# A post-LayerNorm transformer layer with eight experts: results scattered to token rows, side steps dealt by counted DVE work, POOL and SP in emission order, LayerNorm stores from ACT

## The chip, the core and the metric

The kernel runs on one core of one Trainium2 chip. The metric is the device time of one execution in microseconds (us); several executions were timed and their median is given. One further execution was recorded by the hardware profiler; its page and its trace are what is read here. PE is the tensor engine, DVE the vector engine, ACT the scalar engine, POOL is GpSimd and SP the engine that mostly issues DMAs. "SPq" is the queue of SP's sequencer.

## The reference

The input holds 16 sequences of 512 tokens with 128 features. All arithmetic is float32.

```python
Q, K, V = heads(x @ Wq.T + bq), heads(x @ Wk.T + bk), heads(x @ Wv.T + bv)   # 16 heads of 8
probs = softmax(Q @ K.T / sqrt(8))
intervened = probs.at[:, :, :, 0].set(0.0); intervened /= intervened.sum(-1)
attn = ((probs + 0.5 * (intervened - probs)) @ V) @ Wo.T + bo
x1 = layernorm(x + attn)                              # no scale, no shift
logits = x1 @ gate_w.T                                # 8 experts
w, selected = phi_routing(logits)                     # two experts and two weights a token
moe = sum over e of wte[:, e] * ((silu(x1 @ w1[e].T) * (x1 @ w3[e].T)) @ w2[e].T)   # F = 512
out = layernorm(x1 + moe)
```

## The kernel before

**Turns.** A sequence ("batch" b) takes 32 turns (UNITS). A turn n handles one pair of score blocks. `scores` writes transposed scores into a pair of PSUM banks: L388 adds the negated row maxima by a bf16 matmul, L393 adds the products of queries and keys. `exponentials` (L404, ACT) makes `ex` from them, and `weighted` (L413, PE) multiplies `ex` with the values. The row maxima are made LEAD = 20 turns ahead: `maxima` (L338, PE) computes the scores a first time in another pair of banks, and `reduce_maxima` (L346, DVE) reduces them to `nm`. Every 16 turns `put_maxima` splits 16 turns' `nm` into bf16 pieces, transposes them and stores them from `mT` to the operand `mt` (L372).

**Side steps.** Everything else of the attention is written as Python generators that are walked a step further in each turn, up to a `yield`: `load_x`, `project` (queries and keys, high and low parts `hi` and `lo`, stored to `qrow` and `krow` in DRAM, L290), `load_operands` (loads `qt` and `kt`, L322), `values`, `after_attention` (division by the denominators, output matrix, LayerNorm, store of `x1d` at L468), `route` (logits, the two chosen experts, their weights, and the places of the tokens within the experts' lists) and `finish`. Each generator in the list `active` makes one step a turn; of those that need a PSUM bank of their own (`ONE`) only the first does.

**Experts.** The batches form groups of 3, 4, 4, 3 and 2. `route` ends with eight indirect DMAs per batch (L615), two a turn, that scatter the rows of `x1` into `xg`, ordered by expert. When the last batch of a group is through, `plan` computes from the counts which expert and which rows each tile of 128 rows has, and for every token the row of its two results (`yrow`). `experts` then walks the group's tiles, 163 in all: `fetch` loads the expert's weights `ws` (768 KB, L695) and the rows `xs` (64 KB, L697) three tiles ahead (AHEAD) at addresses read from `plan`'s result; `up` multiplies (L111), `activate` makes `th` and `hT` (L716, L720, L724), and `down_and_turn` multiplies tile j down and transposes tile j+2's rows (L115) into the same bank; ACT copies both to `yx` (L749). Tile j's half goes to `yg` by a DMA from SP:

```python
            if j >= 0:
                nc.sync.dma_start(grp.yg[j * P : (j + 1) * P, :], yx[:, 0, :])
```

**Finish.** When a group's tiles are done, `finish` runs per batch: eight indirect DMAs from POOL (L785), two a turn, gather the two results of each token into `yt`; `xr` is loaded from `x1d`; two DVE operations per quarter (L797, L800) make the weighted sum `z`; then LayerNorm and the store of `out` (L807). LayerNorm (L233 to L251) runs on DVE but for one POOL power (L245, `lnrs`) and the final ACT activations (L251).

**What sets the order.** PE, DVE and ACT execute in the order in which the Python code emits. POOL and SP are ordered by the framework's scheduler, which chose, for instance, to start the copy of the expert weights into one array (`wcat`, three DMAs) near the start of the program although it is emitted in turn 48. How many expert instructions a turn gets is a goal in columns of matmul: what is left of the group, divided by the turns up to its due turn `until` (with CHAIN = 32 and WAIT = 8), plus BASE = 1450. After the last turn ("the tail") only the last group has a goal of its own, half a tile a pass.

Of the kernel before, what the change touches and what calls it, by code (L numbers as in the profile page):

```python
# [33 lines left out]
def post_ln_layer(  # L34
# [78 lines left out]

    def turned(out, src, identity):
        nc.tensor.transpose(out, src, identity)  # L115
        dealt[0] += P
# [43 lines left out]
    nc.vector.tensor_copy(ident_b, ident)  # L160
# [3 lines left out]
    nc.vector.memset(keymask, 1.0)  # L164
    nc.vector.memset(keymask[0:1, :], 0.0)
# [3 lines left out]
    for i in range(2):  # L169
# [3 lines left out]
        nc.vector.tensor_scalar(  # L173
# [5 lines left out]
    for e in range(E):  # L179
        nc.vector.memset(revidx[:, e : e + 1], float(E - e))  # L180
    mhalf = const.tile([P, NT], F32, name="mhalf")
    nc.vector.memset(mhalf, -0.5)
# [5 lines left out]
    def concat_weights():  # L188
        rows = wcat.rearrange("(e p) c -> p e c", p=P)
        nc.sync.dma_start(rows[:, :, 0:F], w1T)  # L190
        nc.sync.dma_start(rows[:, :, F : 2 * F], w3T)
        nc.sync.dma_start(rows[:, :, 2 * F : WROW], w2T.rearrange("p e c d -> p e (c d)"))
# [9 lines left out]

    before = const.tile([P, P], F32, name="before")
# [5 lines left out]
    zeros = const.tile([P, 512], F32, name="zeros")  # L209
# [4 lines left out]
    nc.vector.memset(ones8, 1.0)  # L214
    zero8 = const.tile([P, E], F32, name="zero8")
    nc.vector.memset(zero8, 0.0)
    edge = const.tile([P, JT], F32, name="edge")
    for j in range(JT):
        nc.vector.memset(edge[:, j : j + 1], float(j * P))
    kidx = const.tile([P, KT], F32, name="kidx")  # L220
    for k in range(KT):
        nc.vector.memset(kidx[:, k : k + 1], float(k))
# [3 lines left out]
    nc.vector.tensor_copy(pidx, pidx_i)  # L226
# [5 lines left out]

    def layernorm(dst, z, tag):  # L233
# [3 lines left out]
        for t in range(NT):  # L237
            nc.vector.bn_stats(st[:, t, :], z[:, t, :])
            if t % 2 == 1:
                yield None  # L240
        for t in range(NT):
            nc.vector.bn_aggr(mv[:, t, :], st[:, t, :])
        rs = small.tile([P, NT], F32, tag="lnrs", name=f"lnrs{tag}")
        nc.vector.tensor_scalar_add(rs, mv[:, :, 1], LN_EPS)
        nc.gpsimd.tensor_tensor(rs, rs, mhalf, ALU.pow)  # L245
        yield None
        yield None
        off = small.tile([P, NT], F32, tag="lnoff", name=f"lnoff{tag}")
        nc.vector.scalar_tensor_tensor(off, mv[:, :, 0], -1.0, rs, ALU.mult, ALU.mult)
        for t in range(NT):  # L250
            nc.scalar.activation(  # L251
                dst[:, t, :], z[:, t, :], AF.Identity, bias=off[:, t : t + 1],
# [8 lines left out]
    TURN = "turn"  # L261
    SCORE = 680
# [4 lines left out]
    def project(b):  # L267
# [11 lines left out]
        for i, rows in enumerate(qkrows[b]):  # L279
# [6 lines left out]
            nc.vector.scalar_tensor_tensor(  # L286
# [5 lines left out]
    def values(b):  # L292
# [10 lines left out]
        nc.vector.tensor_tensor(  # L303
# [6 lines left out]
        nc.vector.tensor_scalar(  # L310
# [33 lines left out]
    def reduce_maxima(ks, nm):  # L344

        nc.vector.tensor_reduce(nm, pair(ks), AX.X, ALU.max, negate=True)  # L346
        release(*ks)

    def put_maxima(b, half):

        yield None
        nm = nms.pop((b, half)).rearrange("p t s j -> p t j s")
        pc = small.tile([P, NT, 4, NPC, 2], BF16, tag="pc", name=f"pc{b}_{half}")
        for r in range(NPC):
            nc.vector.tensor_copy(pc[:, :, :, r, :], nm)
            if r < NPC - 1:
                rest = small.tile([P, NT, 4, 2], F32, tag="rest", name=f"rest{b}_{half}_{r}")
                nc.vector.tensor_tensor(rest, nm, pc[:, :, :, r, :], ALU.subtract)
# [628 lines left out]
```

## Time and profile before

| | |
|---|---|
| Time, median of 3 runs | 1698.61 us (1688.18 to 1700.37) |
| Time of the profiled execution | 1850.96 us |
| Span of the profiled execution | 1849.2 us |
| Mean granted TensorE clock in it | 0.850 |
| PE busy | 1457.5 us, 79% of the span |
| DVE busy | 1130.0 us, 61% |
| ACT busy | 854.6 us, 46% |
| POOL busy | 347.1 us, 19% |
| Bytes moved | 276.35 MB, mean 149 GB/s |

The profiled execution is longer than the timed ones. Busy time is the time in which an engine executes instructions; a busy engine is not at its peak. The page cuts the span into 40 slices of about 46 us and gives each engine's busy share in tenths. In the groups, a row has the line, engine and operation, what is written from what, the shape and the count, then busy us in all and mean ns of one, and then the idle time in front of these instructions with what ended most of it. In the list of waits a row has the waiting engine and line, what it waited for, and us in all, how often, and the longest. In the trace the first `ex` starts at 55.84 us, the last turn ends near 1627, and the last result of an expert tile is copied at 1812.4.

### The profile page before, as it was taken

To read this page: it belongs to the slowest core of one execution; us is meant where nothing else is said; L and a number is where in the kernel's file an instruction comes from. 1 tells how busy PE (TensorE), PEld (TensorE's weight loads), DVE (VectorE), ACT (ScalarE), POOL (GpSimd) and SP (SyncE) were. 2 spreads that over 40 slices of the span, in tenths; PEclk is the share of its full clock that TensorE was granted. 3 is DMA by queue.
4 is the path that set the end of the run, shared out by engine and by line. 5 is a ranking of instruction groups with operands and counts; after the bars stand their busy time and mean duration, and the time that the engine had idled before them with its cause. 6 is when DMAs were issued, how large, how long until landed. Compare 5 with 4: busy or idle time off the path is not lost.

```text
span 1849.2 us, 28501 instructions
## 1 busy us (share of the span) xinstructions
PE 1457.5 (79%) x10283; PEld 850.2 (46%) x10283; DVE 1130.0 (61%) x2264; ACT 854.6 (46%) x1270; POOL 347.1 (19%) x352
## 2 busy tenths in 40 slices
PE   4788887778979798788879798888859977977671
PEld 1223232234545454444545454554535545667661
DVE  5656665666767676565657677566656764345342
ACT  1355554545556564354546464454535544432221
POOL 2000102111010101222210101222230014123324
PEclk9557776779999997888879898889988998988996
DMA  8761212245353442445445443455544524556671
GB/s 292 274 228 35 86 45 71 89 138 169 107 171 119 157 143 78 150 138 169 144 139 168 143 150 107 148 170 188 164 134 149 180 94 154 175 172 214 220 247 59
DMA packets 137820, 276.35 MB, mean 149 GB/s; under 512 B 17232, under 2 KB 60496, under 8 KB 137680
## 3 DMA queue, kind: packets, MB, share of 16 engines
q1 hardware_dynamic: 129488, 257.74, 42.8%
q0 software_dynamic: 8192, 16.79, 3.0%
q8 instruction: 81, 1.33, 0.3%
q14 instruction: 59, 0.48, 0.1%
HBM read 195.89 MB, written 84.08 MB: 151 GB/s over the span
## 4 chain that ended last, share of the span: by engine, by line
PE 51%; DVE 20%; issue 9%; ACT 7%; another core or an unknown queue 5%; DMA 4%; POOL 3%; SPq 1%; POOLq 0%; ACTq 0%; DVEq 0%
PE banks L111 22%; PE banks L413 12%; DVE nm L346 10%; PE banks L388 7%; PE banks L338 5%; PE banks L115 4%; ACT ex L404 3%; PE banks L393 2%; POOL yt L785 2%; DMA xs<-xg 1%; DVE th L720 1%; ACT y L251 1%; ACT x L251 1%; DVE hT L724 1%
## 5 line engine op out<-in xcount | busy, mean ns | idle before, releaser
L346 DVE TENSOR_REDUCE nm<-banks 128x2 f32<-128x1024 f32 x512 | 624.5, 1222 | 486.7 <-PE banks L338 321.9
L404 ACT ACTIVATE ex<-banks 128x1024 f32<-128x1024 f32 x512 | 524.1, 1024 | 462.6 <-PE banks L393 358.7
L111 PE MATMUL banks<-yx,ws 128*128 128x128 f32 x2608 | 405.3, 301 | 40.6 <-ACT yx L749 16.5
L111 PEld LDWEIGHTS banks<-yx,ws 128*128 128x128 f32 x2608 | 349.4, 207 | 183.9 <-issue 139.2
L338 PE MATMUL banks<-kt,qt 32*128 32x512 f32 x1024 | 290.6, 568 | 89.0 <-DVE nm L346 61.6
L393 PE MATMUL banks<-qt,kt 32*128 32x512 f32 x1024 | 332.1, 643 | 0.0
L413 PE MATMUL banks<-ex,vaug 128*32 128x512 f32 x2048 | 322.7, 707 | 0.0
L388 PE MATMUL banks<-mt,ones_b 3*128 3x512 bf16 x1024 | 225.4, 434 | 61.8 <-issue 21.0
L615 POOL DMA_INDIRECT xg<-x,sloti x128 | 126.4, 987 | 511.3 <-DVE lo L286 122.0
L111 PE MATMUL banks<-ws,hT 128*128 128x128 f32 x1304 | 194.9, 298 | 5.6 <-ACT aw L431 3.5
L111 PEld LDWEIGHTS banks<-ws,hT 128*128 128x128 f32 x1304 | 184.5, 217 | 10.2 <-ACT aw L431 6.2
L785 POOL DMA_INDIRECT yt<-yg,yrow x128 | 132.3, 1034 | 284.2 <-DVE z L800 89.5
L388 PEld LDWEIGHTS <-ones_b 3*128 3x128 bf16 x1024 | 56.4, 94 | 252.0 <-issue 210.5
L716 ACT ACTIVATE th<-banks 128x512 f32<-128x512 f32 x163 | 97.0, 595 | 159.1 <-PE banks L111 111.8
L338 PEld LDWEIGHTS banks<-kt,qt 32*128 32x128 f32 x1024 | 107.1, 207 | 128.4 <-DVE nm L346 91.2
L724 DVE TENSOR_TENSOR hT<-th,banks 128x512 f32<-128x512 f32 x163 | 111.0, 681 | 62.3 <-PE banks L111 43.7
L720 DVE SCALAR_TENSOR_TENSOR th<-th,banks 128x512 f32<-128x512 f32 x163 | 110.8, 680 | 60.2 <-ACT th L716 57.0
L749 ACT COPY yx<-banks 128x256 f32<-128x256 f32 (+1 forms) x178 | 62.6, 352 | 172.4 <-PE banks L111 131.8
L115 PE MATMUL banks<-ident,xs 128*128 128x128 f32 x163 | 53.4, 328 | 82.9 <-ACT mT L369 29.2
L393 PEld LDWEIGHTS banks<-qt,kt 32*128 32x128 f32 x1024 | 110.0, 211 | 0.0
L413 PEld LDWEIGHTS banks<-ex,vaug 128*32 128x32 f32 x2048 | 42.9, 115 | 87.5 <-issue 86.4
L115 PEld LDWEIGHTS banks<-ident,xs 128*128 128x128 f32 x163 | 24.5, 150 | 126.2 <-ACT mT L369 31.3
(128 smaller groups left out, 1001.4 us busy)
## 6 DMA issues: line engine op xcount, KB each, us to landing
ws<-wcat SPq DMA_DIRECT2D x163, 768.0 KB
qt<-qrow SPq DMA_DIRECT2D x32, 512.0 KB
kt<-krow SPq DMA_DIRECT2D x32, 512.0 KB
xg<-zeros SPq DMA_DIRECT2D x16, 1024.0 KB
xs<-xg SPq DMA_DIRECT2D x163, 64.0 KB
yg<-yx SPq DMA_DIRECT2D x163, 64.0 KB
qrow<-hi SPq DMA_DIRECT2D x32, 256.0 KB
qrow<-lo SPq DMA_DIRECT2D x32, 256.0 KB
```

What stands on the lines that cost most here:

```text
L111: nc.tensor.matmul(out, lhsT, rhs, start=start, stop=stop)
L115: nc.tensor.transpose(out, src, identity)
L338: nc.tensor.matmul(pm[:, u, :], qt[at, s, t * P : (t + 1) * P], kt[at, s, :], start=True, stop=True)
L346: nc.vector.tensor_reduce(nm, pair(ks), AX.X, ALU.max, negate=True)
L388: nc.tensor.matmul(pc[:, u, :], ones_b[at : at + NPC, :], mt[at : at + NPC, g % 2, :], start=True, stop=False,)
L393: nc.tensor.matmul(pc[:, u, :], kt[at : at + HR, g % 2, c * P : (c + 1) * P], qt[at : at + HR, g % 2, :], start=False, stop=True,)
L404: nc.scalar.activation(ex, pair(ks), AF.Exp, scale=SCALE)
L413: nc.tensor.matmul(av[32 * j : 32 * j + 32, :], vas[b][:, c, 4 * g + j, :], ex[j // 2][:, j % 2, :], start=(c == 0), stop=(c == NT - 1),)
L615: put = nc.gpsimd.indirect_dma_start(out=grp.xg, out_offset=bass.IndirectOffsetOnAxis(ap=sloti[:, s, t : t + 1], axis=0), in_=x1[:, t, :], ...
L720: nc.vector.scalar_tensor_tensor(th, th, 1.0, banks[:, ks[0], :], ALU.add, ALU.mult)
L724: nc.vector.tensor_tensor(hT, th, banks[:, ks[1], :], ALU.mult)
L785: nc.gpsimd.indirect_dma_start(out=yt[:, s, t, :], out_offset=None, in_=grp.yg, in_offset=bass.IndirectOffsetOnAxis(ap=grp.yrow[:, i, s, t ...
```

## The change

1. **Results.** The array `yg` and the indices `yrow` are gone. `xg` has two more columns (XW = 130), which POOL copies into `x1`: twice the token's number within the group (`token`), and its first expert. `plan` computes three marks per tile instead. When a tile's rows are turned, two POOL operations make from these columns the row of `yd` that each result belongs to (token times two, plus one where the tile is of the first expert; rows past an expert's count go to places of nobody), and `put_results` scatters the tile by one indirect DMA from POOL. `finish` loads its batch's 512 KB of `yd` by one plain DMA from SP.
2. **Side steps.** All DVE operations of the kernel go through `Counted`, which adds up their free size plus 150 each. A side step is walked when the DVE work emitted so far is less than FULL = 2400 ahead of what the turns have served, or when it has waited more than PATIENCE = 3 turns (1 for the last batch of a group), or when its kind is exempt. `xg`'s indirect DMAs go one a turn (`yield POOL`). `plan` is cut into steps.
3. **Order.** POOL and SP execute in emission order too. The copy into `wcat` is cut in three, emitted in turns 24, 28 and 32; the second array of `xg` is cleared in turns 40 to 68.
4. **Stores** of `x1d` and `out` are issued by ACT.
5. **Constants.** WAIT 8 becomes 4, CHAIN 32 becomes 42; after the last turn every group has half a tile a pass as its goal, and urgent generators step twice.

The replacement of `nc.vector` by `dve` is left out below.

```diff
+    class Counted:
+        ISSUE = 150
+        walked = 0
+        def __getattr__(self, name):
+            op = getattr(nc.vector, name)
+            def counted(*args, **kwargs):
+                wide = max(a[:].free_size() for a in args if hasattr(a, "shape"))
+                self.walked += wide + self.ISSUE
+                return op(*args, **kwargs)
+            return counted
...
-    def concat_weights():
+    def concat_weights(part):
         rows = wcat.rearrange("(e p) c -> p e c", p=P)
-        nc.sync.dma_start(rows[:, :, 0:F], w1T)
-        nc.sync.dma_start(rows[:, :, F : 2 * F], w3T)
-        nc.sync.dma_start(rows[:, :, 2 * F : WROW], w2T.rearrange("p e c d -> p e (c d)"))
+        w = (w1T, w3T, w2T.rearrange("p e c d -> p e (c d)"))[part]
+        nc.sync.dma_start(rows[:, :, part * F : (part + 1) * F], w)
...
# after_attention
+        nc.gpsimd.tensor_copy(x1[:, :, D], token[:, b - grp.first, :])
         yield from layernorm(x1, z, f"a{b}")
-        nc.sync.dma_start(grp.x1[b - grp.first], x1.rearrange("p t d -> p (t d)"))
+        nc.scalar.dma_start(
+            grp.x1[b - grp.first].rearrange("p (t d) -> p t d", d=D), x1[:, :, 0:D]
+        )
...
# route
+        nc.gpsimd.tensor_copy(x1[:, :, D + 1], ix[:, 0, :])
...
         for t in range(NT):
-            yield None
             for s in range(2):
+                yield POOL
                 put = nc.gpsimd.indirect_dma_start(
...
# plan
+        step = small.tile([P, E], F32, tag="pl_step", name=f"pl_step{g}")
+        dve.tensor_scalar_mul(step, grp.count, -1.0)
+        dve.tensor_tensor(step[:, 0 : E - 1], step[:, 0 : E - 1], grp.count[:, 1:E], ALU.add)
+        dve.tensor_tensor(steps, past, step.unsqueeze(1).to_broadcast(wide), ALU.mult)
+        dve.tensor_reduce(own, steps, AX.X, ALU.add)
...
+        dve.tensor_scalar(grp.mark[:, 0, :], ek, -1.0, float(E), ALU.mult, ALU.add)
+        dve.scalar_tensor_tensor(
+            grp.mark[:, 1, :], own, grp.count[:, 0:1], jk, ALU.add, ALU.is_gt
+        )
...
# down_and_turn
-                turned(pt[:, D : 2 * D], got[k][1], ident)
+                xs = got[k][1]
+                turned(pt[:, D : 2 * D], xs[:, 0:D], ident)
                 xsTs[k] = yx[:, 1, :]
+                nc.gpsimd.tensor_scalar(
+                    to, xs[:, D + 1 : D + 2], mark[:, 0, :], xs[:, D : D + 1],
+                    ALU.is_equal, ALU.add,
+                )
+                nc.gpsimd.tensor_scalar(
+                    tos[k], to, mark[:, 1, :], mark[:, 2, :], ALU.mult, ALU.add
+                )
...
-                nc.sync.dma_start(grp.yg[j * P : (j + 1) * P, :], yx[:, 0, :])
+                puts.append((yx, tos.pop(j)))
+
+        def put_results():
+            yx, to = puts.pop(0)
+            put = nc.gpsimd.indirect_dma_start(
+                out=grp.yd, out_offset=bass.IndirectOffsetOnAxis(ap=to, axis=0),
+                in_=yx[:, 0, :], in_offset=None,
+                bounds_check=YROWS + tiles_of(CAP) * P - 1, oob_is_err=True,
+            )
...
# experts, ahead of each down_and_turn
+                while puts:
+                    put_results()
                 down_and_turn(k - 2, k + 1)
...
# finish
-        for t in range(NT):
-            yield None
-            for s in range(2):
-                nc.gpsimd.indirect_dma_start(
-                    out=yt[:, s, t, :], out_offset=None, in_=grp.yg,
-                    in_offset=bass.IndirectOffsetOnAxis(ap=grp.yrow[:, i, s, t : t + 1], axis=0),
-                    bounds_check=grp.tiles * P - 1, oob_is_err=True,
-                )
+        yt = work.tile([P, NT, 2, D], F32, tag="yt", name=f"yt{b}", bufs=1)
+        nc.sync.dma_start(
+            yt, grp.yd[i * n : (i + 1) * n, :].rearrange("(p t s) d -> p t s d", t=NT, s=2)
+        )
...
-        nc.sync.dma_start(out[b].rearrange("(p t) d -> p t d", t=NT), y)
+        nc.scalar.dma_start(out[b].rearrange("(p t) d -> p t d", t=NT), y)
...
# the loop over the turns
+            served = min(served + max(1900, (dealt[0] - before_turn) * 4 // 5 + 300), dve.walked)
...
-            taken = False
-            for gen in list(active):
-                if gen.need == ONE:
-                    if taken:
-                        continue
-                    taken = True
-                if not gen.more():
+            gen = next((gen for gen in active if gen.need == ONE), None)
+            order = [gen] if gen else []
+            order += [gen for gen in active if gen.need != ONE]
+            put = False
+            for gen in order:
+                if gen.need == POOL and put:
+                    continue
+                if gen.last is None:
+                    gen.last = turn
+                free = dve.walked - served < FULL or turn >= end
+                late_by = turn - gen.last - (1 if gen.urgent else PATIENCE)
+                if gen.need in (ONE, NOW, POOL, REST) or free or late_by > 0:
+                    put = put or gen.need == POOL
+                    gen.last = turn
+                    if not gen.more():
+                        active.remove(gen)
...
-    with tc.manual_schedule(
-        engines={mybir.EngineType.PE, mybir.EngineType.DVE, mybir.EngineType.Activation}
-    ):
+    with tc.manual_schedule(
+        engines={
+            mybir.EngineType.PE, mybir.EngineType.DVE, mybir.EngineType.Activation,
+            mybir.EngineType.Pool, mybir.EngineType.SP,
+        }
+    ):
```

## The prediction

> **What bounds the kernel now.** I read the page first, for which engine is full and when.
>
> ```profile
> PE 1457.5 (79%) x10283; PEld 850.2 (46%) x10283; DVE 1130.0 (61%) x2264; ACT 854.6 (46%) x1270; POOL 347.1 (19%) x352
> ...
> PE   4788887778979798788879798888859977977671
> ...
> POOL 2000102111010101222210101222230014123324
> PEclk9557776779999997888879898889988998988996
> ...
> PE 51%; DVE 20%; issue 9%; ACT 7%; another core or an unknown queue 5%; DMA 4%; POOL 3%; SPq 1%; POOLq 0%; ACTq 0%; DVEq 0%
> ```
>
> TensorE holds 79% of the span and half of the chain; no other engine is near. Slices 1, 39 and 40 are poor, and POOL is heaviest in the last six. So an edit can win at the two ends, or in the holes of a PE that is otherwise full. The change leaves every matmul (7047 in both programs).
>
> The groups tell who makes the holes.
>
> ```profile
> L346 DVE TENSOR_REDUCE nm<-banks 128x2 f32<-128x1024 f32 x512 | 624.5, 1222 | 486.7 <-PE banks L338 321.9
> ...
> L338 PE MATMUL banks<-kt,qt 32*128 32x512 f32 x1024 | 290.6, 568 | 89.0 <-DVE nm L346 61.6
> ...
> L615 POOL DMA_INDIRECT xg<-x,sloti x128 | 126.4, 987 | 511.3 <-DVE lo L286 122.0
> ...
> L785 POOL DMA_INDIRECT yt<-yg,yrow x128 | 132.3, 1034 | 284.2 <-DVE z L800 89.5
> ```
>
> Each turn needs one nm of 1222 ns; where DVE comes late with it, PE's next L338 waits (61.6 us in all). Then by stage: a batch with finishes, one without, and the tail behind the last turn.
>
> ```profile
> 744.40:863.90 119.50, 94.95 (x627) 54.85 (x627) 67.31 (x130) 52.99 (x80) 29.83 (x29) 0.80 0.45 144
> 1065.30:1158.70 93.40, 80.31 (x618) 47.79 (x619) 67.63 (x130) 50.27 (x73) 11.94 (x12) 0.94 0.42 135
> 1627.00:1849.20 222.20, 136.06 (x1034) 127.76 (x1032) 96.91 (x287) 55.62 (x129) 76.03 (x74) 0.85 0.57 186
> ```
>
> Columns: length, then busy us of PE, PEld, DVE, ACT and POOL, clock, DMA share, GB/s. PE is busy 79%, 86% and 61%. The tail wastes most, and the waits inside it say on what (total, times, longest):
>
> ```profile
> DVE lnofff L249 <- POOL lnrsf L245: 25.2, 7, 6.0
> ...
> DVE z L797 <- DMA yt<-yg,yrow: 12.3, 6, 7.1
> ...
> DVE z L797 <- DMA xr<-x1d: 11.7, 3, 5.5
> ...
> PEld banks L115 <- POOL at L448: 9.5, 1, 9.5
> ...
> DVE z L800 <- DMA yt<-yg,yrow: 7.4, 7, 1.7
> ```
>
> All five come of gathers standing ahead of a one-microsecond power, an addition or a load: 66.1 us in 222.
>
> **The sum, part by part.** The profiled execution took 1851.0 us, its span 1849.2. That is 152 us over the median of the runs, 1698.6, and no row says which rows lengthened. I make the sum in microseconds of the profiled execution and take the same microseconds from the median.
>
> *Start.* The chain opens so:
>
> ```profile
> 6.47 9.90 DMA wcat<-in_w1T
> 16.39 5.18 DMA krow<-lo
> 21.65 5.22 DMA kt<-krow
> ```
>
> The 2 MB copy of weights stands in SP's queue before the first operand stores, because a scheduler placed it. With SP in emission order it goes to turns 24, 28 and 32, where the DMA share is under a half, long before the first expert tile. At most the 9.9 us go; some of the early loads remain: **−8** (0 to −10).
>
> *Side steps on DVE.* I laid the changed DVE order out with the durations of before's rows and summed what stands between two nm's. Beyond 1.0 us a turn it is 110.0 us before and 102.6 after (beyond 0.8: 148.4 and 141.7). The rationing smooths little, since most excess is one 1.2 to 2 us operation, which cannot be split; what does split is plan, 4.9 us in one turn before. **−7** (0 to −15). The 29 more DVE operations lie inside this count: in the attention phase 397.0 us of side work become 395.5, the new marks against the ops for yrow.
>
> *One put a turn.* xg's 8 indirect DMAs of a batch (987 ns) now go one a turn, not in a burst. Near these bursts PE stands still once or twice a batch, 4 to 11 us at a time, about 78 us in all, with no releaser but an unknown queue (5% of the chain). It may be the recording itself, which would also explain part of the 152 us. Ends 0 and −78; nearer to the first, as no recorded instruction waits for a put: **−10**.
>
> *Scatter in place of store and gather.* Gone: 163 stores on SP, 128 gathers on POOL (132.3 us). Added on POOL: 163 scatters, by the nearest row (L785, 1034 ns) 168.5 us, and 326 scalar operations on 128x1; the nearest rows are an iota (126 ns) and a power (1092 ns for 128x4), I take 0.15 us: 49 us. With 32 small copies into the new columns, 5 us, POOL goes from 347 to some 437 us, 24% of the span, all beside PE in the attention phase. Rows of xg grow from 128 to 130 elements: 1.6% more of 64 KB, nothing beside the 768 KB of ws. On SP the store stands in front of the fetches:
>
> ```profile
> SPq L695 <- PE banks L111: 378.5, 83, 13.9
> ...
> SPq L753 <- ACT yx L749: 139.9, 61, 8.2
> ...
> SPq L807 <- ACT y L251: 40.9, 11, 10.7
> ```
>
> L753's 139.9 us of queue time vanish. Fetches lead by 25 to 50 us in the attention phase, so nothing is won there; in the tail they lead by 8 to 10 us only. Here the Trainium skill, "DMA: Bandwidth & Descriptors", section "Issuing engine by pattern", speaks against the change: plain stores belong to Sync, whose hardware path it calls generally faster, and GpSimd is for indirect ones. By the rule alone each result pays the step from 0.33 us of issue (x1d's row) to 1.03 us: 0.7 us on some 43 tail tiles, **+30** if POOL were on the path. By the rows POOL is busy 76.0 of 222.2 us in the tail and its gathers are what is waited for; a scatter waits only for the ACT copy of its own tile, two tiles before anyone reads it. Behind it on POOL stand the same powers and L448, but for one microsecond each and not for a burst of 10.6. I follow the rows: of the 66.1 us of tail waits, two thirds delay something that PE needs or overlap with nothing; half of these 44 us go, **−22** (+10 to −45).
>
> *The end.* After the last tile's result (1812.4) the last two batches need 36.8 us:
>
> ```profile
> 1815.54 1.08 POOL L785 DMA_INDIRECT yt<-yg,yrow  x1 [10.33 <-issue]
> ...
> 1838.54 1.01 POOL L785 DMA_INDIRECT yt<-yg,yrow  x1 [0.30 <-issue]
> ```
>
> Sixteen gathers take 24 us of it. After: one scatter (1.0 plus about 2.5 to land), two loads of 512 KB side by side (5.2 us, as kt's), then z, LayerNorm and store as before, 10 us from the last gather: two batches partly in a row, 23 us. **−13** (−8 to −18).
>
> *Finishes in the attention phase.* Eleven batches finish there; per burst of 10.6 us a power (lnrsa, L448) can be caught behind it. Row: the batch with finishes has 29.8 us of POOL, the one without 11.9. **−5** (0 to −15).
>
> *Stores of LayerNorm from ACT.* On SP each took 0.33 us, plus 18.4 and 40.9 us of queue time waiting for ACT, all of it in front of fetches. On ACT the wait for its own four activations remains and 32 issues of 0.33 us lie in front of ex: 10.6 us at full price. The skill's same page, "Issuing engines are not separate DMA queues", says that spreading issues over engines saves only sequencer time, usually small: by that rule it is a loss of up to 10.6 us. By the rows SP gets 59 us of queue time back, of value only in the tail. **+6** (+20 to −5).
>
> *Balance.* Because of the new constants (CHAIN, WAIT, goal) 43.5 tiles go up after the last turn, 38.75 before. At 3.3 us of PE a tile some 15 us leave the attention phase and 16 enter the tail: **+1**.
>
> *Manual order of POOL and SP.* Nothing overtakes any more: a store that waits for hi or mt now stands before fetches that were ready. Cover: the 25 to 50 us lead, if gone 8 to 14 us a time (L695's longest). **+3** (0 to +40).
>
> Sum: −8 −7 −10 −22 −13 −5 +6 +1 +3 = **−55**. 1851 becomes 1796; the median 1698.6 becomes **1644**.
>
> **Rivals.** One percent (17 us) is about what a measurement of this kernel tells from no change.
> 1. *PE-bound after all* (0.14): the waits removed are filled by tiles that PE must do anyway; only start and end gain, −21, and ACT's stores and the order give back 9: 1687. For: 79% PE. Against: a tail at 61%.
> 2. *The burst stalls are real* (0.17): the whole 78 and not 10 goes: 1644 − 68 = 1576. For: regular stalls at every burst. Against: records are missing there.
> 3. *In-order SP and POOL queues block fetches* (0.15): a store waiting for its producer (L290 and L372 do) holds ws; place: the attention phase, where a tile has an urgent due turn. It decides from the point where the held time exceeds the lead of three tiles (25 us). If one tile in four of 163 then costs 2.5 us, +100, against −55: 1744. For: SP waits 378.5 us behind L695 already. Against: SP loses 163 stores and the 32 of LayerNorm and gains 16 loads, and its order is nearly that of use.
> 4. *Rationing doesn't ration* (inside the forecast): then its −7 is 0 and the time 1651; 148.4 to 141.7 says nearly as much already.
>
> The forecast has 0.54. Its own range, with one or two of its terms at their ends, is 1612 to 1682. **The range** 1570 to 1712 holds rivals 1 and 2 as well; most of rival 3 is left out. Faster by over 1% (under 1681.6): 0.50 of the forecast, rival 2's 0.17 and 0.05 of rival 1, 0.72. Within 1%: the rest of these two, 0.13. Slower: rival 3, 0.15.
>
> **What would show it.** First ex at 47 us, not 55.84; tail waits on POOL and yt under 25 us; last scatter to end under 26 us; PE idle near puts gone if rival 2; PE in the batch 1065 to 1158 still 80 us; SP's waits on ACT gone. The forecast fails if tail PE stays at 61%, or if PE waits for DMA ws grow in the attention phase.

## The result, and the profile after

The changed kernel ("after") takes 1688.4 us, median of 20 runs, and the kernel before 1699.5 us, median of 20. The ratio is 0.9936, interval 0.991 to 0.9963: 11 us are won, where 55 were forecast.

One thing must be known to read the numbers below. Runs fell on chips of two kinds: on one, before takes 1699 us; on the other 1830 to 1841 us, and the recording that the prediction was read from (1851 us) fits only the second. So every ratio below is against before on the same chip, and "kind 1699" or "kind 1840" stands beside it; on kind 1840 after is at 0.934, interval 0.927 to 0.941 (median of all its runs 1708.5 us, of before's 1837.5). So the same change won 0.6% on the one kind and 6.6%, some 120 us, on the other; the forecast of 55 us fits neither.

The page of after, with the lines that answer to the first ones shown of before: busy time, slices, chain.

```profile
PE 1409.0 (84%) x10283; PEld 824.0 (49%) x10283; DVE 1135.0 (68%) x2293; ACT 853.6 (51%) x1270; POOL 513.6 (31%) x745
...
PE   4778888888899988989998998899999999777762
...
POOL 2000202021242323322434242423434343544443
PEclk7677675767999989999999999899999989888996
...
PE 48%; DVE 18%; DMA 14%; issue 8%; ACT 6%; POOL 4%; SPq 1%; ACTq 1%; POOLq 0%; DVEq 0%
PE banks L111 19%; PE banks L447 11%; DVE nm L126 11%; DMA yd<-yx,toi 10%; PE banks L422 7%; PE banks L372 5%; PE banks L133 4%; ACT ex L438 2%; PE banks L427 2%; POOL xg L654 1%; DMA kt<-krow 1%; ACT x L282 1%; DVE z L126 1%; ACT y L282 1%; DVE th L126 1%
```

The turns are denser, slices 35 to 40 are not, and DMA rose from 4% to 14% of the chain. Nearly all of that is one item that did not exist before, the scatter `yd<-yx,toi`, with 10%. (All DVE operations now have line 126, that of `Counted`, so DVE is read by tiles.)

For a fair comparison before was recorded again, on kind 1699 (`b_again`, 1696.9 us). By stage, the turns and then the tail, of `b_again` and then of after; columns are start and end, length, busy us of PE, PEld (PE's weight loads), DVE, ACT and POOL with counts, clock, DMA share, GB/s:

```profile
56.20:1477.30 1421.10, 1234.72 (x9168) 676.33 (x9169) 1000.58 (x1874) 791.52 (x1132) 261.20 (x258) 0.90 0.48 154
1477.30:1696.90 219.60, 138.07 (x1046) 129.57 (x1041) 96.68 (x287) 56.72 (x130) 76.03 (x74) 0.83 0.59 191
```

```profile
52.60:1433.20 1380.60, 1228.36 (x9055) 664.78 (x9057) 997.74 (x1881) 786.04 (x1125) 398.82 (x567) 0.89 0.48 161
1433.20:1676.10 242.90, 156.45 (x1158) 149.46 (x1150) 103.30 (x300) 61.77 (x138) 106.06 (x159) 0.83 0.58 193
```

The start is 3.6 us shorter, the turns 40.5 us, the tail 23.3 us longer: 20.8 us between these two recordings. The tail's own PE work grew by 18.4 us, since about four more tiles lie in it, as was forecast; but the largest of the waits that were to shrink there did not. Here are the tail's waits in after (total, times, longest):

```profile
POOL toi L791 <- DMA yd<-yx,toi: 79.3, 39, 5.0
...
DVE lnofff L126 <- POOL lnrsf L276: 28.2, 7, 8.4
PEld banks L111 <- ACT yx L804: 25.1, 6, 6.6
...
PEld banks L133 <- DMA xs<-xg: 19.2, 10, 5.3
...
DVE z L126 <- DMA xr<-x1d: 9.8, 2, 8.1
...
PEld banks L133 <- POOL at L482: 7.4, 1, 7.4
```

The gathers are gone, and still `lnoff` waits 28.2 us for its power and PE 7.4 us for an addition on POOL (`at`). What holds POOL stands in the first line: the operation that writes a row number, `toi`, waits for a scatter, in 39 of the tail's 43 tiles, and 315.1 us over the whole kernel:

```profile
L812 POOL DMA_INDIRECT yd<-yx,toi x163 | 170.0, 1043 | 198.5 <-ACT yx L804 153.3
...
L791 POOL TENSOR_SCALAR toi<-to,mark 128x1 int32<-128x1 f32 x163 | 58.1, 356 | 317.3 <-DMA yd<-yx,toi 315.1
```

The cause is in the code. `toi` has four buffers. In step k `put_results` issues the scatter of tile k-3, and straight after it `down_and_turn` writes the row number of tile k+1, which is four tiles on and takes that same buffer. The buffer is given free only when the scatter has landed, so POOL stands still until the DMA it has just issued is done. One such stretch of the tail, from the timeline (start us, length, engine, line, what; in brackets the idle time before it and what ended it):

```profile
1535.47 1.06 POOL L812 DMA_INDIRECT yd<-yx,toi  x1 [0.36 <-issue]
...
1536.58 0.38 POOL L786 TENSOR_SCALAR to<-xs,mark 128x1 f32<-128x1 f32 x1
1536.98 0.33 SPq L740 DMA_DIRECT2D xs<-xg  x1
1538.30 0.34 POOL L791 TENSOR_SCALAR toi<-to,mark 128x1 int32<-128x1 f32 x1 [1.35 <-DMA yd<-yx,toi]
1538.60 1.04 POOL L276 TENSOR_TENSOR lnrsf<-lnrsf,mhalf 128x4 f32<-128x4 f32 x1
1539.67 0.16 DVE L126 SCALAR_TENSOR_TENSOR lnofff<-lnmvf,lnrsf 128x4 f32<-128x4 f32 x1 [6.39 <-POOL lnrsf L276]
1539.84 1.09 POOL L812 DMA_INDIRECT yd<-yx,toi  x1 [0.20 <-issue]
1539.87 1.65 ACT L282 ACTIVATE y<-z,lnofff,lnrsf 128x128 f32<-128x128 f32 x4 [6.48 <-DVE lnofff L126]
...
1542.43 0.37 ACT L804 COPY yx<-banks 128x256 f32<-128x256 f32 x1
1542.85 1.44 PE L111 MATMUL banks<-yx,ws 128*128 128x128 f32 x5 [5.88 <-ACT yx L804]
```

Read it downwards: `toi` waits for the scatter, the power stands behind `toi`, `lnoff` has waited 6.39 us for the power, `y` 6.48 us for `lnoff`, `yx` stands behind `y` on ACT, and PE has been idle 5.88 us. There is a second way out of the same delay: SP issues the next `xs` 0.4 us after `to` has started, because `to` reads the old `xs`. From scatter to scatter it is 4.37 us, while the forecast counted 3.3 us of PE for a tile.

### The profile page after: what moved, and what is told of

The parts are those of the page before. It is cut to its first block, busy times and chain, and to the rows that moved or that the text cites. A ratio compares the mean times of both kernels' runs of the same rounds, so it can differ in the third digit from the quotient of the medians.

```text
span 1676.1 us, 28734 instructions
## 1 busy us (share of the span) xinstructions
PE 1409.0 (84%) x10283; PEld 824.0 (49%) x10283; DVE 1135.0 (68%) x2293; ACT 853.6 (51%) x1270; POOL 513.6 (31%) x745
## 4 chain that ended last, share of the span: by engine, by line
PE 48%; DVE 18%; DMA 14%; issue 8%; ACT 6%; POOL 4%; SPq 1%; ACTq 1%; POOLq 0%; DVEq 0%
PE banks L111 19%; PE banks L447 11%; DVE nm L126 11%; DMA yd<-yx,toi 10%; PE banks L422 7%; PE banks L372 5%; PE banks L133 4%; ACT ex L438 2%; PE banks L427 2%; POOL xg L654 1%; DMA kt<-krow 1%; ACT x L282 1%; DVE z L126 1%; ACT y L282 1%; DVE th L126 1%
## 5 line engine op out<-in xcount | busy, mean ns | idle before, releaser
L111 PE MATMUL banks<-yx,ws 128*128 128x128 f32 x2608 | 390.3, 294 | 35.6 <-ACT yx L804 29.7
L111 PEld LDWEIGHTS banks<-yx,ws 128*128 128x128 f32 x2608 | 339.2, 202 | 146.9 <-issue 100.4
L372 PE MATMUL banks<-kt,qt 32*128 32x512 f32 x1024 | 283.5, 554 | 77.3 <-DVE nm L126 59.8
L427 PE MATMUL banks<-qt,kt 32*128 32x512 f32 x1024 | 321.4, 625 | 0.0
L447 PE MATMUL banks<-ex,vaug 128*32 128x512 f32 x2048 | 315.1, 691 | 0.0
L812 POOL DMA_INDIRECT yd<-yx,toi x163 | 170.0, 1043 | 198.5 <-ACT yx L804 153.3
L111 PE MATMUL banks<-ws,hT 128*128 128x128 f32 x1304 | 184.9, 288 | 3.9 <-ACT aT L491 2.1
L111 PEld LDWEIGHTS banks<-ws,hT 128*128 128x128 f32 x1304 | 174.7, 207 | 8.1 <-ACT aT L491 2.6
L372 PEld LDWEIGHTS banks<-kt,qt 32*128 32x128 f32 x1024 | 104.4, 202 | 120.1 <-DVE nm L126 95.5
L791 POOL TENSOR_SCALAR toi<-to,mark 128x1 int32<-128x1 f32 x163 | 58.1, 356 | 317.3 <-DMA yd<-yx,toi 315.1
L126 DVE TENSOR_TENSOR hT<-th,banks 128x512 f32<-128x512 f32 x163 | 110.9, 680 | 52.2 <-PE banks L111 51.0
L786 POOL TENSOR_SCALAR to<-xs,mark 128x1 f32<-128x1 f32 x163 | 63.1, 387 | 63.7 <-DMA xs<-xg 56.7
```

The costliest lines, as they stand in the source:

```text
L111: nc.tensor.matmul(out, lhsT, rhs, start=start, stop=stop)
L126: return op(*args, **kwargs)
L372: nc.tensor.matmul(pm[:, u, :], qt[at, s, t * P : (t + 1) * P], kt[at, s, :], start=True, stop=True)
L427: nc.tensor.matmul(pc[:, u, :], kt[at : at + HR, g % 2, c * P : (c + 1) * P], qt[at : at + HR, g % 2, :], start=False, stop=True,)
L447: nc.tensor.matmul(av[32 * j : 32 * j + 32, :], vas[b][:, c, 4 * g + j, :], ex[j // 2][:, j % 2, :], start=(c == 0), stop=(c == NT - 1),)
L786: nc.gpsimd.tensor_scalar(to, xs[:, D + 1 : D + 2], mark[:, 0, :], xs[:, D : D + 1], ALU.is_equal, ALU.add,)
```

## The experiments

**More row-number buffers, `a_toi8`.** The one wait is taken away.

```diff
-                to = small.tile([P, 1], F32, tag="to", name=f"to{g}_{k}", bufs=4)
+                to = small.tile([P, 1], F32, tag="to", name=f"to{g}_{k}", bufs=8)
...
-                tos[k] = small.tile([P, 1], mybir.dt.int32, tag="toi", name=f"toi{g}_{k}", bufs=4)
+                tos[k] = small.tile([P, 1], mybir.dt.int32, tag="toi", name=f"toi{g}_{k}", bufs=8)
```

> After, with eight buffers instead of four for the row numbers to and toi: the POOL operation that writes them (toi) no longer waits for the scatter issued just before it, which it does for 315 us in after's trace. If this wait, and the POOL work that stands behind it, costs time: 5 to 20 us less than after (ratio to before 0.982 to 0.990), mostly behind the last turn. If POOL has slack everywhere: as after, 0.990 to 0.997, the 315 us gone and PE's gaps unchanged.

Measured, kind 1699: 1633.9 us, ratio 0.963 (0.9587 to 0.9672). That is 54.5 us less than after, more than was expected of the wait. Its stages, turns and tail:

```profile
52.60:1427.90 1375.30, 1224.66 (x9056) 662.33 (x9057) 997.18 (x1881) 785.91 (x1125) 400.67 (x571) 0.90 0.48 161
1427.90:1618.60 190.70, 141.70 (x1158) 135.68 (x1150) 103.10 (x300) 61.58 (x138) 103.38 (x156) 0.89 0.71 246
```

The busy time of DVE, ACT and POOL is nearly the same, and the tail is 52.2 us shorter. PE is busy 14.8 us less there for the same matmuls, at a granted clock of 0.89 instead of 0.83. `lnoff` waits 4.9 us there instead of 28.2, and no wait of `toi` for a scatter is left.

**A second run of the same, and of after, `t_again` and `a_again`**, to have both on kind 1840.

> a_toi8 (after with eight buffers for to and toi), unchanged. On a chip of the 1699 kind: 0.959 to 0.967 again. On one of the 1841 kind: about 0.925 to 0.935, if t_oldgoal (0.944) and t_sched (0.949) lost 1 to 2% by what they undo; 0.944 or more, if they lost nothing.

> After, unchanged, beside the others of this group: the last group ran on a chip on which before takes 1841 us and not 1699, so its kernels lack a partner. If this chip is of the 1699 kind: ratio to before 0.990 to 0.998 as known. If of the 1841 kind: what a_gather (0.965) and a_xs6 (0.932) say depends on it; the scatter with its wait costs nothing if after is 0.965 here, and gains or loses the difference otherwise.

Measured, kind 1840: 0.905 (0.899 to 0.911) and 0.934 (0.927 to 0.941). From after to `a_toi8` it is 3.1% by these ratios, and 0.963 / 0.9936 gives 3.1% on kind 1699 too: this wait costs about the same on both kinds, while before does not take the same time on both.

**Five buffers, `a_toi5`.** `bufs=5` in the same two lines.

> After with five buffers instead of four for to and toi. With four, toi of tile k+1 takes the buffer of the scatter issued just ahead of it; with five, that of the one a tile earlier, 4 us old. A scatter lands about 2.3 us after its issue, so theory E expects all of a_toi8's gain: 0.903 to 0.910 on the 1841 kind of chip, 0.961 to 0.967 on the 1699 kind, POOL's waits for DMA yd under 15 us. If the gain came of something else in the memory layout of eight buffers: between 0.915 and 0.934.

Measured, kind 1840: 0.9083 (0.904 to 0.9126). One buffer more is enough, within the interval; what is left of the wait is, in the tail,

```profile
POOL toi L791 <- DMA yd<-yx,toi: 22.1, 20, 2.6
```

and 34.7 us over the whole kernel, where under 15 were expected and after has 315.1. So it is the one scatter just ahead, not the layout of eight buffers.

**Which way POOL's wait reaches PE: `a_xs6`, `a_recip`, `a_both`.** These leave the wait and close its ways out. `a_xs6` gives `xs` six buffers; `a_recip` takes the power off POOL and puts a reciprocal on DVE, without the square root, so it does not compute LayerNorm and serves for its time alone; `a_both` does both.

```diff
-        xs = work.tile([P, XW], F32, tag="xs", name=f"xs{g}_{k}", bufs=3)
+        xs = work.tile([P, XW], F32, tag="xs", name=f"xs{g}_{k}", bufs=6)
```

```diff
-        nc.gpsimd.tensor_tensor(rs, rs, mhalf, ALU.pow)
+        dve.reciprocal(rs, rs)
```

> After, with six buffers instead of three for xs, and still four for toi. In after's tail each xs fetch is issued 0.4 us after the POOL operation to, which reads the old xs, and to stands behind the toi that waits for its scatter. Theory C (the wait is paid through the fetch: late POOL frees xs late, SP issues xs and ws late, PE waits): most of the 55 us of a_toi8 comes back without touching toi, ratio to before 0.96 to 0.975. Theory D (it is paid through the power lnrs, which stands behind toi on POOL and holds DVE's lnoff, ACT's y and with them yx): little comes back, 0.988 to 0.995, the lnoff waits stay near 28 us in the tail. Both: in between.

> After, still with four buffers for toi, but LayerNorm's power on POOL is replaced by a reciprocal on DVE (it leaves out the square root, for the time alone). Theory D (toi's wait reaches PE through the power that stands behind it on POOL): most of what a_toi8 won comes back: 0.910 to 0.920 of before on a chip of the 1841 kind, 0.965 to 0.978 on one of the 1699 kind. Theory C (through the xs and ws fetches): as after, 0.934 or 0.994. a_xs6 was as after, which speaks for D. POOL's toi still waits over 200 us for DMA yd under both.

> After with six xs buffers and the reciprocal on DVE (it leaves out the square root, for the time alone) together; toi keeps four buffers and waits for its scatter as before. Theory E (POOL's loop of scatter, landing, toi and to is the pace of the tail, and leaves through whichever path is open: lnoff waits went from 27 to 44 us when xs was freed, xs waits from 18 to 35 when the power was taken off): with both doors shut 0.905 to 0.915 of before on the 1841 kind of chip, 0.963 to 0.972 on the 1699 kind, unless ACT's yx, whose buffer the scatter reads, becomes a third door, then 0.92 to 0.93. If POOL's wait matters in another way: as a_recip and a_xs6, 0.929 to 0.934.

Measured, kind 1840, beside after's 0.934: `a_xs6` 0.9317 (0.925 to 0.9383), `a_recip` 0.9292 (0.927 to 0.9314), `a_both` 0.9349 (0.9301 to 0.9397). None gains what `a_toi8` gains (0.905). The tails' waits show why. First `a_xs6`:

```profile
POOL toi L791 <- DMA yd<-yx,toi: 86.9, 38, 5.6
...
PEld banks L111 <- ACT yx L804: 52.2, 10, 13.6
...
DVE lnofff L126 <- POOL lnrsf L276: 43.7, 5, 12.3
```

The `xs` waits (19.2 us in after) are gone from its list, those for `lnoff` grew from 28.2 to 43.7 and PE's for `yx` from 25.1 to 52.2. Then `a_recip`:

```profile
POOL toi L791 <- DMA yd<-yx,toi: 87.0, 38, 5.3
...
PEld banks L133 <- DMA xs<-xg: 35.0, 21, 4.6
...
ACT yx L804 <- DMA yd<-yx,toi: 12.5, 4, 4.6
```

No `lnoff` waits any more, but `xs` waits of 35.0. And `a_both`:

```profile
POOL toi L791 <- DMA yd<-yx,toi: 90.1, 37, 5.3
...
ACT yx L804 <- DMA yd<-yx,toi: 51.8, 22, 6.9
PEld banks L111 <- ACT yx L804: 41.2, 20, 9.0
```

A third way carries it: `yx` has four buffers too, the scatter reads them, and ACT waits 51.8 us for one. So theories C and D were both wrong as alternatives, and the waits are those of E: POOL's loop is the pace of the tail, and whichever way is closed, the next one carries the delay. In size E missed: with the third way open it expected 0.92 to 0.93, and 0.9349 is no gain at all.

**Before, recorded once more, `b_again`.**

> The kernel before, unchanged, recorded a second time. The recorded execution of before took 1851 us where its timed ones take 1699, while the one of after took 1676 beside 1688. Theory A (something in before is slowed only while it is recorded, the bursts of indirect DMAs): again 1830 to 1870 us, with PE standing still 4 to 11 us at the same bursts. Theory B (that one recording was a disturbed execution): about 1690 to 1710 us.

The number is that of theory B, 1696.9 us, and the stalls at the bursts are not there. But `b_again` ran on kind 1699, and the first recording fits only kind 1840, so this does not show that the first was a disturbed execution. The nearest kernel recorded on kind 1840 is `b_newgoal`, before with other goals (below). Here are two of the waits of the first recording, then the same of `b_newgoal`; `remote` stands for a releaser that the profile does not show:

```profile
DVE nm L346 <- remote: 73.5, 18, 10.9
ACT ex L404 <- remote: 64.0, 19, 6.3
```

```profile
ACT ex L404 <- remote: 69.7, 17, 8.3
...
DVE nm L346 <- remote: 52.6, 12, 7.7
```

The stalls are back, and `b_again` has no such row. Ahead of each of these waits of over 1 us, 52 in the first recording and 39 in `b_newgoal`, at least five indirect DMAs of POOL start within 15 us. One burst of `b_newgoal`:

```profile
725.16 0.71 PE L111 MATMUL banks<-yx,ws 128*128 128x128 f32 x4
725.41 0.97 POOL L615 DMA_INDIRECT xg<-x,sloti  x1 [0.31 <-issue]
726.68 0.97 POOL L615 DMA_INDIRECT xg<-x,sloti  x1 [0.30 <-issue]
727.96 0.97 POOL L615 DMA_INDIRECT xg<-x,sloti  x1 [0.31 <-issue]
729.23 0.97 POOL L615 DMA_INDIRECT xg<-x,sloti  x1 [0.30 <-issue]
729.91 1.23 DVE L346 TENSOR_REDUCE nm<-banks 128x2 f32<-128x1024 f32 x1 [5.13 <-remote]
730.68 1.02 ACT L404 ACTIVATE ex<-banks 128x1024 f32<-128x1024 f32 x1 [7.85 <-remote]
```

For 4 us PE, DVE and ACT all stand still beside the scatters. Missing records are not the reason: before, `b_again` and `b_newgoal` have the same count of instructions on each of the three engines. So the stalls belong to kind 1840 together with bursts. On kind 1699 the same bursts leave no such wait (`b_again`, `b_manual`, `a_burst`); on kind 1840 the kernel with one put a turn, `t_again`, has none for `nm` and 4.9 us for `ex`. What holds the engines stays open. Of the 152 us between the two recordings of before, PE is busy 60.4 us more, for the same matmuls at a granted clock of 0.850 instead of 0.884; in the other 92 it is idle.

**Bursts, `a_burst`.** Eight puts in one step.

```diff
+        yield POOL
         for t in range(NT):
             for s in range(2):
-                yield POOL
                 put = nc.gpsimd.indirect_dma_start(
```

> After, with the eight puts of a batch in one step instead of one a turn. Theory A (bursts stall only while recorded): timed within 0.4% of after (ratio to before 0.990 to 0.998), but the profiled execution 30 to 80 us longer than after's 1676, with PE gaps of 4 to 6 us at the bursts. Rival 2 of the prediction (bursts stall always): timed 1.02 to 1.05 of after. No effect at all: both as after.

Measured, kind 1699: 0.995 (0.9922 to 0.9978), recorded 1682.5 us. Like after on both counts: one put a turn is worth nothing that can be measured there, and rival 2 of the prediction falls for that kind. Kind 1840, where before's bursts do stall, was not tried with this edit.

**Order alone, `b_manual`.** Before with POOL and SP in emission order (the last hunk of the diff, alone).

> Before, with POOL and SP in emission order and nothing else changed: the indirect DMAs are then emitted two a turn, and the copy into wcat leaves the start. If order alone carries the gain (start and no overtaking): ratio 0.990 to 0.996. If in-order queues hold fetches behind stores that wait (rival 3): above 1.00, up to 1.03. Theory A for the recording: its profiled span falls well under 1800 us, because the gathers no longer come as eight in a row.

Measured, kind 1699: 1.0062 (1.0038 to 1.0085), a loss of 0.6%. The first `ex` comes at 51.9 us and not 56.2, so the start gains 4.3 us, and more than that is lost later, the way rival 3 pointed; which waits lost it was not followed up.

**Order undone, `t_sched` and `t_sched2`.** `a_toi8` without `Pool` and `SP` in the list of engines, twice.

> a_toi8 (after with eight buffers for to and toi) with POOL and SP left to the scheduler again. b_manual alone was 0.6% slower than before, so if the fixed order costs here as well: 0.5 to 1% faster than a_toi8 (ratio to before 0.953 to 0.958). If the fixed order suits the new steps (stores and puts dealt over the turns): 0.3 to 1.5% slower than a_toi8, 0.966 to 0.978, start 4 us later because wcat comes first.

> t_sched (a_toi8 with POOL and SP ordered by the scheduler) once more. On the 1841 kind of chip it was 4.8% slower than a_toi8. If this chip is of the 1699 kind and the loss belongs to the order: 0.98 to 1.01 of before. If the loss belongs to that chip: 0.963 to 0.970.

Measured, kind 1840 both times: 0.9489 (0.9438 to 0.954) and 0.9485 (0.9462 to 0.9508), 4.8% over `a_toi8`. On that kind the fixed order is worth 4.8% with the new steps. Its recordings show part of the reason: the scheduler draws a batch's eight puts together again, within 10.1 us in the median batch against 17.7 in `t_again`, and the stalls of before return:

```profile
ACT ex L438 <- remote: 51.8, 14, 6.2
...
DVE nm L126 <- remote: 40.7, 11, 6.2
```

Whether the order is worth anything on kind 1699, where bursts do not stall, stayed open, since no run of it fell there.

**Goals, `t_oldgoal` and `b_newgoal`.** `a_toi8` with the old goals, and before with the new ones; the diff of the first:

```diff
-    WAIT = 4
+    WAIT = 8
-    CHAIN = 42
+    CHAIN = 32
...
-                if turn >= end:
+                if turn >= end and gen.grp.g == len(GROUPS) - 1:
                     goal = TILE // 2
```

> a_toi8 with the old goals: CHAIN 32, WAIT 8, and half a tile a pass after the last turn for the last group only. Prediction: 43.5 tiles lie behind the last turn with the new goals, 38.75 with the old; at 3.3 us of PE a tile what leaves the tail enters the turns: within 0.4% of a_toi8 (0.959 to 0.967). If the turns have no room for the tiles: 0.5% faster with the new goals, so 0.968 or more here. If they do have room: 0.955 or less.

> Before, with the new goals alone: WAIT 4, CHAIN 42, half a tile a pass for every group after the last turn. The prediction gave this part +1 us, and t_oldgoal lost 4% against a_toi8 on the 1841 kind of chip. If the goals are worth that by themselves: 0.96 to 0.985. If only together with dealt steps and the scatter: 0.995 to 1.005. If the tail, still with gathers, is too slow for four tiles more: above 1.005.

Measured, kind 1840: `t_oldgoal` 0.944 (0.938 to 0.950), 4.3% over `a_toi8`; `b_newgoal` 0.9955 (0.9912 to 0.9997). On this kind the goals alone give about half a percent, with the rest some nine times that. The loss is in the turns: 1482.4 us against 1400.0 of `t_again`, with PE busy 1277.1 us against 1230.4 for nearly the same count, at a granted clock of 0.85 against 0.89. The recordings of `t_sched` and `t_sched2` show the same lower clock, 0.85 and 0.86 in the turns. Whether it is the cause or follows from stalls was not settled; of the stalls at puts `t_oldgoal` has few (10.6 us of `nm`, 20.3 of `ex`).

**Rationing off, `t_nodeal`.**

```diff
-    FULL = 2400
+    FULL = 1000000000
```

> a_toi8 with the rationing off (FULL so large that every side step is walked when its turn comes; puts still one a turn). Prediction: rationing is worth 7 us (0 to 15): ratio to a_toi8 1.000 to 1.009, with the waits of PE L372 for nm rising from 53 us towards 62. If it is worth nothing: 0.997 to 1.003 of a_toi8. If it delays chains more than it smooths: below 0.997.

Measured, kind 1840: 0.9188 (0.9128 to 0.9248), 1.5% over `a_toi8`, more than the 7 us forecast. The wait that it was to shorten, L372 for `nm`, went the expected way (62.3 us, and 55.1 in `t_again`), but that is 7 of the 28 us; the rest has no row that I can name.

**Stores, `t_sp_store`.** `nc.scalar` back to `nc.sync` in the two stores of LayerNorm.

> a_toi8 with LayerNorm's stores x1d and out issued by SP again. Prediction: ACT's issue costs 6 us (from -5 to 20), so this is 0.3% faster, 0.988 to 1.003 of a_toi8. Rival, the store on SP waits for ACT's y and holds the fetches behind it in the tail (40.9 us of such queue time in before): 1.003 to 1.02 of a_toi8, with PE waits for ws or xs of over 10 us more in the tail.

Measured, kind 1840: 0.9045 (0.898 to 0.9111) beside 0.905: no difference. Neither the 6 us of cost nor the rival's gain is there.

**The end, `t_xr`.** `xr` is loaded ahead of `yt`.

```diff
+        nc.sync.dma_start(xr.rearrange("p t d -> p (t d)"), grp.x1[i])
         nc.sync.dma_start(
             yt, grp.yd[i * n : (i + 1) * n, :].rearrange("(p t s) d -> p t s d", t=NT, s=2)
         )
-        nc.sync.dma_start(xr.rearrange("p t d -> p (t d)"), grp.x1[i])
```

> a_toi8 with the load of xr emitted ahead of the load of yt in finish. With SP in emission order xr now stands behind yt, which waits for the scatters; at the end of after the chain shows 3.5 and 3.7 us of DMA xr. If these are on the path: 3 to 7 us less than a_toi8, 0.995 to 0.998 of it (0.901 to 0.904 of before on the 1841 kind of chip, 0.959 to 0.961 on the 1699 kind). If not: as a_toi8.

Measured, kind 1840: 0.9045 (0.9014 to 0.9075), as `a_toi8`. `z` needs `yt` just as much, and `yt` lands no sooner.

**The scatter undone, `a_gather`.** After with the store to `yg`, `plan`'s `yrow` and the gathers, one a turn.

```diff
-                puts.append((yx, tos.pop(j)))
+                nc.sync.dma_start(grp.yg[j * P : (j + 1) * P, :], yx[:, 0, :])
...
-        nc.sync.dma_start(
-            yt, grp.yd[i * n : (i + 1) * n, :].rearrange("(p t s) d -> p t s d", t=NT, s=2)
-        )
+        for t in range(NT):
+            for s in range(2):
+                yield POOL
+                nc.gpsimd.indirect_dma_start(
+                    out=yt[:, s, t, :], out_offset=None, in_=grp.yg,
...
```

> After without part 1: results stored to yg by SP and gathered in finish by eight indirect DMAs from POOL, one a turn; everything else of the change stays. If the scatter as built is what takes the gain back: faster than after, ratio to before 0.972 to 0.985, no POOL wait on DMA yd. If the scatter gains in spite of its wait: slower than after, 0.997 to 1.01, with the 24 us of gathers at the end again.

Measured, kind 1840: 0.965 (0.9603 to 0.9697), 3.3% over after. This says less than it seems. In its recording the end behind the last `th` takes 87 us, in after 35: the gathers of five batches came to stand there one batch after another, some 15 us each. That pile is of my dealing of the gathers and was not in before (41 us). Taking those 52 us off, about 0.937 would be left, as after's 0.934. That is worked out, not measured, and the recording has stalls at bursts as well (25.3 us of `nm` for `remote`, in 7 places). So what the scatter is worth in place of store and gather is not shown, with its wait or without.

## Why the prediction was right or wrong

**The step that failed** is in the part on the scatter: "a scatter waits only for the ACT copy of its own tile, two tiles before anyone reads it". That is true of the scatter. But of what the change added I priced the two scalar operations by their length and never asked what they wait for. They write a buffer that is free only when the scatter has landed; `bufs=4` in the new lines told it. With −22 for the waits, −13 for the end and +16 for the tiles moved in, the forecast had the tail 19 us shorter; it got 23.3 us longer, and `a_toi8` shows 52.2 us of tail in this one wait.

**The rule that I set aside was nearer.** I weighed the Trainium skill, "DMA: Bandwidth & Descriptors", section "Issuing engine by pattern" (plain stores to Sync, indirect ones to GpSimd), which by price made +30 us "if POOL were on the path", and followed the rows, since POOL was busy only a third of the tail. POOL was on the path of the tail: 106.1 us busy and 79.3 us waiting in 242.9. A share of busy time did not tell it, because in-order waiting is not busy time. But the reason was not the rule's either: with one more buffer (`a_toi5`) the same scatters, from the same engine and as long, are rid of nearly all of the wait.

**Sizes.** The two scalar operations took 387 and 356 ns and not 150; POOL is busy 513.6 us and not 437. That did no harm by itself: `a_toi8` has the same lengths.

**Start:** −8 forecast, −3.6 measured. The copy into `wcat` left the chain, but first loads and SP's own issue took part of its place.

**Turns:** the terms there (−7 for rationing, −10 for puts, −5 for finishes, −15 for tiles moved, +6 and +3) make −28; the recordings of kind 1699 show −40.5. The total came near by luck, for the parts did not: puts are nothing on kind 1699, and stores on ACT are nothing on kind 1840; undone from the whole on kind 1840, rationing is worth 1.5%, goals 4.3% and order 4.8%, all more than their terms, while alone the goals gave 0.5% there and order lost 0.6% on kind 1699. These parts depend on each other and on the chip.

**Balance:** 43.5 tiles behind the last turn were forecast; 43 are there. **End:** the piece from the last `th` to the end went from 40.5 to 35.2 us, 5 and not 13. The gathers are gone, but the last scatters and the loads of `yt` and `xr` behind them stand on the chain. The 11.7 us of waits for `xr` were counted among those that come of gathers; they do not, for without gathers they are 9.8 us in after and 10.4 in `a_toi8`.

**Two readings** of no weight: the 7047 matmuls stand in no recording, while both count 10283 on PE, so that the edit leaves them, as was said; and slice 39, called poor, has PE at seven tenths.

**A second step that failed** is "I make the sum in microseconds of the profiled execution and take the same microseconds from the median". The recording was of kind 1840 and the median of kind 1699; the gap of 152 us was seen, and "the recording itself" was put forward for it. On kind 1699 the burst stalls do not exist, so that their term, −10, is 0 there. On kind 1840 they are real, and there the change won 6.6%: rival 2, with its 78 us, had 7.2%, the forecast 3.2%. That rival 2 comes so near is in part luck, since it did not know of the scatter's wait either, and how much of the 6.6% the puts are was not tried apart. The forecast of 1644 us is 10 us off the kernel without the wait (1633.9), which is no merit of a sum that did not know of the wait.

**A better version** than both kernels is `a_toi8`: 0.963 of before on kind 1699, 0.905 on kind 1840.

## What to carry to other kernels

When a change moves work to an in-order engine, count for every added instruction what it waits for, its buffer's last reader among them; an index buffer was free here only when the indirect DMA that reads it had landed (315.1 us of waits), so it needs one buffer more than the distance in tiles between the scatter just issued and the number written next (four here, and `a_toi5` shows that five do). When an engine's loop sets the pace, closing the path by which its delay is seen only makes another path show it: three different waits carried the same delay here, and only the loop's own wait was worth removing. And when an execution is recorded 9% over its timed median, ask whether both ran on the same chip before microseconds of the one are taken from the other; the stalls it shows may be real where it ran.

## What was not expected of the hardware

A TENSOR_SCALAR of 128x1 on POOL takes 356 to 387 ns, while a copy of 128x4 takes 193 to 203. An indirect DMA holds its issuing engine 1.04 us, then needs about 1.8 us more until it lands: `toi` started 2.83 us after the scatter did. On kind 1840, PE, DVE and ACT stand still for some microseconds beside a burst of indirect DMAs from POOL, and on kind 1699 beside the same burst they do not. The same program differs by 8% between chips (1699 and 1840 us for before), while `a_toi8` differs by 1.1% (1633.9 and 1651.9): the margin between two kernels that is measured on one chip need not be that of another.
